# Reordering VectorE's sums in a seven-product projection, and moving the next image's GroupNorm statistics one attention group later

## The chip, the cores and the metric

One core of a Trainium2 chip. Its engines here are TensorE (matrix products, which it writes to the memory PSUM), VectorE (sums and products element by element), ScalarE (exponentials and copies) and GpSimd; transfers to and from the chip's main memory are called DMA. The metric is the device time of one execution in microseconds (us). All runs used here are within 1.5% of the fastest of their kernel and count as fast, at a granted TensorE clock of 0.995 to 0.999 of full speed. Numbers are medians of several executions unless they come from a trace, which is one execution; the span of a trace is about 2 us shorter than the time of the same execution.

## The reference, cut

Eight images of 512 x 32 x 32 in fp32. Each is normalised over groups of channels, goes through a 1x1 convolution, two blocks (3x3 convolution, attention with four heads over 1024 positions, 1x1 convolution), a final 1x1 convolution, and a residual sum.

```python
def bot_attention(x, qkv_w, rw, rh):
    qkv = conv2d(x, qkv_w, 0).reshape(b, 3, HEADS, HD, hw)
    q, k, v = (qkv[:, 0], qkv[:, 1], qkv[:, 2])
    r = (rw + rh).reshape(1, HEADS, HD, hw)                 # position sums
    logits = einsum('bhdi,bhdj->bhij', q, k + r) * HD ** -0.5
    out = einsum('bhij,bhdj->bhdi', softmax(logits), v)
# ...
x = x + conv_block(_gn(x), ...)                             # _gn: GroupNorm, the "statistics"
```

## The kernel before

The projection to q, k and v uses seven products of half-size blocks rather than eight (`project_strassen`), in 14 of the 16 blocks (images 1 to 7). Products go to PSUM; VectorE combines them. The part that matters is its end, where `ps_c`, `ps_d`, `ps_e` are PSUM tiles of a ring of three that the logits also use:

```python
product(ps_c, ps_w[:, 0], s2, t2)
tt(u[:, 0:2], ps_c, u[:, 0:2], ALU.add)
tt(u[:, 2], ps_w[:, 0], u[:, 2], ALU.add)
tt(k1, k1, u[:, 1], ALU.add)                      # reads no PSUM
add_r(0, 1)                                       # two position sums, read no PSUM
product(ps_d, ps_w[:, 1], s3, t3)
tt(k2, ps_d[:, 1], u[:, 1], ALU.add)
tt(q2, ps_d[:, 0], u[:, 0], ALU.add)
tt(v2, v_of(ps_w[:, 1]), v_of(u[:, 2]), ALU.add)
product(ps_e, ps_v[:, 0], block_qkv(n, 1, 1), t4)
tt(k3, k2, m5[:, 1], ALU.add)
tt(q3, q2, m5[:, 0], ALU.add)
tt(v3, v2, v_of(m5[:, 2]), ALU.add)               # reads no PSUM
tt(k2, k2, ps_e[:, 1], ALU.subtract)
freed = tt(q2, q2, ps_e[:, 0], ALU.subtract)      # last reader of ps_e
with tc.issue_after(freed.ins):
    tt(v1, v1, v_of(u[:, 2]), ALU.add)
    tt(v2, v2, v_of(ps_v[:, 0]), ALU.subtract)
    tt(q1, q1, u[:, 0], ALU.add)
def later():                                      # the other keys' position sums,
    for half in range(NH): add_r(1, half)         # done inside attention group 0
```

Attention runs in four groups (0 to 3) of eight blocks each: logits (TensorE), exponential (ScalarE), running sum of the exponentials for the softmax (`acc`, VectorE), product with v (TensorE, into `av_ps`, which has one buffer). At the end of a group the row sums go to `s_ps`; their reciprocal travels to memory and back to be spread over the partitions (`r_dram`, `rs`) and scales the output a group later. `behind[g]` is work put behind the first blocks of group g: in the first block of every image but the last, `ahead`:

```python
def ahead():
    g = next(groups)
    next(norm, None)      # a piece of the next image's GroupNorm: statistics, statistics, means, normalisation
    # ... loads
    if b == 0:            # image 0 also makes transformed weights for the second block
        if g == 0:
            make(1, 1, [2])
        elif g <= NM:
            make(1, 1, [0], [g - 1])   # the second of these ends with a store of 1 MB
# ...
scale(g, rs)              # ao *= rs, and then the next group's first output block may be read out
```

## Time and profile before

| | before |
|---|---|
| time, median of 6 runs beside the changed kernel | 2373.88 us (2373.83 to 2375.31) |
| span of the trace | 2371.5 us |
| TensorE busy | 2320.6 us (98%) |
| TensorE's waits that the change aims at | 14 x 0.65 in the projections, 6 x 1.01 at group 1 |
| image 0, first block: from its first projection matmul (71.89) to its first matmul after attention (171.5) | 99.6 us |

The prediction below shows the lines for the two waits. The 0.60 us that it counts for an operation is the usual distance between the starts of VectorE's TENSOR_TENSOR operations of 128x512 fp32 in its lines; each of them lasts 0.68 to 0.69 us there. One more place also belongs here, image 0. TensorE there, before, at the start of group 2; the columns are start, duration, engine, line, operation, and in brackets the idle time and what ended it:

```profile
128.92 3.51 PE L687 MATMUL av_ps<-pt,vT 64*64 64x512 f32 x16 [2.12 <-DVE ao L695]
```

and VectorE up to the start of group 3, where the scaling (L761) stands in its queue just before the read-out that TensorE waits for:

```profile
137.45 0.20 DVE L749 RECIPROCAL rc<-sums_all 128x8 f32<-128x8 f32 x1
...
143.90 0.69 DVE L761 TENSOR_TENSOR ao<-ao,rs 128x512 f32<-128x512 f32 x1
```

The block of 16 after the wait of 2.12 us takes 3.51 us rather than the usual 1.95; the granted clock was 0.58, 0.50, 0.50 and 0.71 in the four microseconds from 129.00. The time from the reciprocal to its use is 6.45 us, and TensorE, 1.6 us late from that slow stretch, doesn't wait at group 3 at all. Both facts return later.

### The profile page before, as it was taken

How to read it: one execution, taken by the hardware profiler on the slowest of the kernel's cores; microseconds unless marked ns; L12 is line 12 of the kernel's file. 1: busy time of each engine (PE TensorE's matmuls, PEld its weight loads, DVE VectorE, ACT ScalarE, POOL GpSimd, SP SyncE). 2: the span in 40 equal slices, each digit the busy share in tenths (PEclk: the TensorE clock that was granted, in tenths of full speed). 3: DMA queues.
4: the chain of work that ended last, by engine and by line, in shares of the span. 5: the costliest groups of instructions: out<-in, count | busy, mean ns of one | idle time of the engine just before them, and what ended most of it. 6: DMA issues, size and time to landing. Idle time of an engine off the chain costs nothing.

```text
span 2371.5 us, 36277 instructions
## 1 busy us (share of the span) xinstructions
PE 2320.6 (98%) x14794; PEld 1169.8 (49%) x14794; DVE 1753.1 (74%) x2811; ACT 946.3 (40%) x1246; POOL 88.2 (4%) x305
## 2 busy tenths in 40 slices
PE   7999999999999999999999999999999999999998
PEld 4536346363553636436364453635536354463633
DVE  8867778687786867868688676886767867677774
ACT  1442624435244352534425344253433525325252
POOL 1000000000100001000010000100001000000001
PEclk9999999999999999999999999999999999999999
DMA  7412234030430305303151131611207021160202
GB/s 251 152 53 89 95 104 194 15 129 15 148 151 15 130 15 186 117 10 129 33 212 74 31 108 33 257 33 54 86 28 262 28 85 55 34 228 16 85 11 69
DMA packets 93069, 226.39 MB, mean 95 GB/s; under 512 B 27872, under 2 KB 49312, under 8 KB 80224
## 3 DMA queue, kind: packets, MB, share of 16 engines
q1 hardware_dynamic: 81376, 174.71, 21.4%
q0 software_dynamic: 11520, 49.29, 5.2%
q8 instruction: 118, 1.93, 0.3%
q14 instruction: 55, 0.45, 0.1%
HBM read 190.41 MB, written 33.55 MB: 94 GB/s over the span
## 4 chain that ended last, share of the span: by engine, by line
PE 82%; DVE 14%; DMA 2%; issue 1%; ACT 0%; SPq 0%; DVEq 0%; POOL 0%; ACTq 0%
PE av_ps L687 16%; PE l_ps L661 14%; PE c_ps L879 13%; PE ps L343 10%; PE c L934 8%; PE c_new L934 6%; PE p_ps L556 5%; PE m_ps L900 5%; DVE acc L673 3%; PE pv_ps L560 2%; DVE st L443 1%; PE s_ps L705 1%; DVE acc L671 1%; DVE u_z L607 1%; DVE kr L577 1%
## 5 line engine op out<-in xcount | busy, mean ns | idle before, releaser
L665 ACT ACTIVATE pt<-l_ps 128x1024 f32<-128x1024 f32 x512 | 496.4, 1022 | 431.4 <-PE l_ps L661 420.1
L673 DVE TENSOR_TENSOR acc<-acc,pt 128x1024 f32<-128x1024 f32 x384 | 469.8, 1223 | 102.1 <-ACT pt L665 78.4
L687 PE MATMUL av_ps<-pt,vT 64*64 64x512 f32 x4096 | 486.6, 593 | 10.7 <-DVE ao L695 10.7
L661 PE MATMUL l_ps<-q,kr 64*64 64x512 f32 x4096 | 487.4, 591 | 9.1 <-DVE q L624 9.1
L879 PEld LDWEIGHTS c_ps<-v_in,u 128*128 128x128 f32 x2720 | 306.3, 192 | 7.9 <-issue 6.7
L879 PE MATMUL c_ps<-v_in,u 128*128 128x128 f32 x2720 | 306.9, 275 | 1.1 <-DVE v_in L400 1.1
L687 PEld LDWEIGHTS av_ps<-pt,vT 64*64 64x64 f32 x4096 | 152.1, 133 | 288.2 <-issue 221.2
L661 PEld LDWEIGHTS l_ps<-q,kr 64*64 64x64 f32 x4096 | 152.3, 133 | 283.4 <-issue 253.1
L343 PE MATMUL ps<-x,w 128*128 128x512 f32 x512 | 226.4, 598 | 2.2 <-DVE x L477 2.2
L343 PEld LDWEIGHTS ps<-x,w 128*128 128x128 f32 x512 | 96.7, 191 | 129.9 <-issue 126.6
L671 DVE TENSOR_TENSOR acc<-pt 128x1024 f32<-128x1024 f32 x64 | 78.3, 1223 | 64.7 <-ACT pt L665 64.7
L407 ACT COPY m<-c_ps 128x256 f32<-128x256 f32 x96 | 35.5, 370 | 224.7 <-PE c_ps L879 219.7
L934 PE MATMUL c_new<-t_in,ws 128*128 128x512 f32 x288 | 124.6, 592 | 0.0
L900 PE MATMUL m_ps<-ao,m_sb 128*128 128x512 f32 x256 | 112.5, 592 | 0.0
L328 ACT ACTIVATE m_kept<-m_kept,bh,sh 128x512 f32<-128x512 f32 x42 | 31.9, 806 | 146.0 <-DVE m_kept L1018 86.3
L761 DVE TENSOR_TENSOR ao<-ao,rs 128x512 f32<-128x512 f32 x64 | 44.1, 689 | 60.8 <-DMA rs<-r_dram 60.2
L934 PEld LDWEIGHTS c_new<-t_in,ws 128*128 128x128 f32 x288 | 54.7, 190 | 68.9 <-issue 66.0
L328 ACT ACTIVATE t<-m_ps,bh,sh 128x512 f32<-128x512 f32 x64 | 48.0, 776 | 83.9 <-PE m_ps L900 82.5
L556 PE MATMUL p_ps<-t_z,sq 128*128 128x512 f32 x168 | 81.3, 593 | 0.0
L372 POOL MEMSET w_rows<- 128x16 f32 x96 | 12.2, 128 | 1821.1 <-PE s_ps L705 1127.9
L900 PEld LDWEIGHTS m_ps<-ao,m_sb 128*128 128x128 f32 x256 | 48.6, 190 | 61.2 <-issue 61.2
L328 ACT ACTIVATE z<-z,bh,sh 128x512 f32<-128x512 f32 x64 | 48.6, 806 | 50.9 <-DVE z L436 50.9
(223 smaller groups left out, 2701.0 us busy)
## 6 DMA issues: line engine op xcount, KB each, us to landing
u<-u SPq DMA_DIRECT2D x85, 1024.0 KB
x<-in_x_dram SPq DMA_DIRECT2D x32, 512.0 KB
x_res<-in_x_dram POOLq DMA_DIRECT2D x28, 512.0 KB, 7.9
out_dram<-m_kept POOLq DMA_DIRECT2D x28, 512.0 KB, 7.4
w<-in_cv_w_dram SPq DMA_DIRECT2D x13, 1024.0 KB
u<-u_new POOLq DMA_DIRECT2D x12, 1024.0 KB, 6.0
rs<-r_dram SPq DMA_DIRECT2D x96, 128.0 KB
ws<-s SPq DMA_DIRECT2D x24, 512.0 KB
```

The source lines that it names most:

```text
L328: return nc.scalar.activation(dst, src, AF.Silu, scale=sh[:, k : k + 1], bias=bh[:, k : k + 1])
L343: nc.tensor.matmul(ps[:, half, :], w_of(k), rhs_of(k, half), start=(k == begin), stop=(k == end))
L556: nc.tensor.matmul(ps[:, o, :], w[:, o, :], rhs, start=not onto, stop=True, skip_group_check=onto)
L560: nc.tensor.matmul(v[:, ts(j, P)], rhs[:, ts(j, P)], w[:, 2, :], start=j == 0 and not onto, stop=True, skip_group_check=True,)
L661: nc.tensor.matmul(ps[kh * HD : (kh + 1) * HD, hd, :], kr[r, c, o : o + HD], q[r, c, ts(half, HALF)], start=True, stop=True,)
L665: exp = nc.scalar.activation(pt[:, i], ps, AF.Exp, scale=SCALE)
L671: return nc.vector.tensor_tensor(accs[g], pt[:, 0], pt[:, 1], ALU.add)
L673: ins = nc.vector.tensor_tensor(accs[g], accs[g], pt[:, i], ALU.add)
L687: nc.tensor.matmul(avs[g][hd * HD : (hd + 1) * HD, kh, :], vT[r, j, o : o + HD], pt[r, i, hd, :], start=(j == 0), stop=(j == NJ - 1),)
L879: nc.tensor.matmul(ps[:, row, col, :], us[i][:, k, row, SLOT[col], :], vs[i][:, k, row, col, :], start=(k == 0), stop=(k == NM - 1),)
L900: nc.tensor.matmul(pss[oc][:, half, :], m2_sb[:, n, k, ts(oc, P)], ao[:, k, ts(half, HALF)], start=(k == 0), stop=(k == NM - 1),)
L934: nc.tensor.matmul(ps[:, o, :], w[:, k, ts(o, P)], rhs[part][:, c, :], start=(k == 0 and not onto), stop=(k == KB - 1), skip_group_check=onto,
```

## The change

Intent: let the last reader of `ps_e` come as early as possible, so that the logits find their PSUM tile free; and take the statistics out of group 0, where VectorE has the postponed position sums to do, to group 1 and 2, with the means in the middle of group 2. No operation is added or removed.

```diff
             tt(u[:, 2], ps_w[:, 0], u[:, 2], ALU.add)
-            tt(k1, k1, u[:, 1], ALU.add)
-            add_r(0, 1)
             ps_d = big()
# ...
             tt(q3, q2, m5[:, 0], ALU.add)
-            tt(v3, v2, v_of(m5[:, 2]), ALU.add)
             tt(k2, k2, ps_e[:, 1], ALU.subtract)
             freed = tt(q2, q2, ps_e[:, 0], ALU.subtract)
             with tc.issue_after(freed.ins):
+                tt(v3, v2, v_of(m5[:, 2]), ALU.add)
+                last = tt(v2, v2, v_of(ps_v[:, 0]), ALU.subtract)
+            with tc.issue_after(last.ins):
+                tt(k1, k1, u[:, 1], ALU.add)
+                add_r(0, 1)
                 tt(v1, v1, v_of(u[:, 2]), ALU.add)
-                tt(v2, v2, v_of(ps_v[:, 0]), ALU.subtract)
                 tt(q1, q1, u[:, 0], ALU.add)
# ... attention: work may also be put behind a later pair of blocks
-                    if j0 == 0:
-                        with tc.issue_after(added.ins):
-                            behind.get(g, lambda: None)()
+                    with tc.issue_after(added.ins):
+                        behind.get(g if j0 == 0 else (g, j0 // PAIR), lambda: None)()
# ... ahead()
-            next(norm, None)
+            if g > 0:
+                next(norm, None)
# ...
+        behind[NG - 2, 2] = lambda: next(norm, None)
```

## The prediction

> **What bounds the kernel now.** I read the page first, then the waits of TensorE, then the timeline of TensorE and VectorE around the places where TensorE waits.
>
> ```profile
> span 2371.5 us, 36277 instructions
> ...
> PE 2320.6 (98%) x14794; PEld 1169.8 (49%) x14794; DVE 1753.1 (74%) x2811; ACT 946.3 (40%) x1246; POOL 88.2 (4%) x305
> ```
>
> TensorE is busy for 2320.6 of 2371.5 us, at a granted clock of 0.997. The change takes no matmul away, so all it can win is idle time of TensorE: 50.9 us, 2.1% of the span. A gain of over 2% is nearly excluded by this line alone. The waits of TensorE name the idle time:
>
> ```profile
> PE gm_ps L449 <- DVE mv L444: 11.8, 1, 11.8
> PE av_ps L687 <- DVE ao L695: 10.7, 11, 2.1
> PE l_ps L661 <- DVE q L624: 9.1, 14, 0.7
> ```
>
> (Columns: microseconds in total, times, longest.) The first is the start of the program and stays. The other two are what the change aims at. The third comes once in each of the 14 projections that use seven products (images 1 to 7, two each). Of the second, the timeline shows six of exactly 1.01 us, always where group 1 of attention follows group 0 in an image that prepares a next one (images 1 to 6, first block); three in image 0 (0.49, 2.12 and 0.63); and two after slow transfers (0.63, 0.77).
>
> Image 2, TensorE at the end of the projection:
>
> ```profile
> 679.93 1.05 PE L560 MATMUL pv_ps<-qkv_sb,t_z 128*128 128x128 f32 x8
> 680.92 1.95 PE L661 MATMUL l_ps<-q,kr 64*64 64x512 f32 x16
> 683.51 1.95 PE L661 MATMUL l_ps<-q,kr 64*64 64x512 f32 x16 [0.65 <-DVE q L624]
> 685.28 1.90 PE L687 MATMUL av_ps<-pt,vT 64*64 64x512 f32 x16
> 687.00 1.90 PE L661 MATMUL l_ps<-q,kr 64*64 64x512 f32 x16
> ```
>
> and VectorE there:
>
> ```profile
> 676.65 0.68 DVE L609 TENSOR_TENSOR kr<-kr,u_z 128x512 f32<-128x512 f32 x1
> 677.37 0.69 DVE L577 TENSOR_TENSOR kr<-kr,rw_sb 128x512 f32<-128x512 f32 x1
> 677.98 0.68 DVE L615 TENSOR_TENSOR kr<-p_ps,u_z 128x512 f32<-128x512 f32 x1
> 678.58 0.68 DVE L578 TENSOR_TENSOR kr<-kr,rh_sb 128x512 f32<-128x512 f32 x1
> ...
> 681.58 0.68 DVE L622 TENSOR_TENSOR vT<-vT,m_z 128x512 f32<-128x512 f32 x1
> 682.18 0.68 DVE L623 TENSOR_TENSOR kr<-kr,p_ps 128x512 f32<-128x512 f32 x1
> 682.78 0.68 DVE L624 TENSOR_TENSOR q<-q,p_ps 128x512 f32<-128x512 f32 x1
> ```
>
> The reader is to see a buffer wait, not a data wait. The second block of logits writes a PSUM tile (three rotate) whose last reader is the subtraction of L624, which ends at 683.46; the block starts at 683.51. Ahead of that reader stand four operations that read no PSUM tile that anyone waits for: L609, L577, L578 and L622. Undisturbed blocks of 16 follow each other by 1.72 us (685.28, 687.00), here the distance is 2.59 and the next one 1.77, so the stall costs 2.59 + 1.77 - 2 x 1.72 = 0.92 us, more than the 0.65 of the wait row, which subtracts a modelled end.
>
> Boundary of groups 0 and 1 in the same image, VectorE then TensorE:
>
> ```profile
> 691.38 1.88 DVE L443 BATCH_NORM_STATS2 st<-x 128x6 f32<-128x512 f32 x3
> ...
> 700.09 0.68 DVE L695 TENSOR_TENSOR ao<-av_ps,ao 128x512 f32<-128x512 f32 x1
> ```
>
> ```profile
> 699.18 0.64 PE L705 MATMUL s_ps<-acc,ones 128*32 128x256 f32 x8
> 700.83 1.95 PE L687 MATMUL av_ps<-pt,vT 64*64 64x512 f32 x16 [1.01 <-DVE ao L695]
> ```
>
> The attention output has one PSUM buffer, so group 1 waits until L695 has read group 0's. VectorE comes late because group 0 holds both the postponed sums of the keys (L577 and L578, four operations, 2.4 us) and the first statistics (2.7 us). Where nothing delays, the output block follows the sums by 0.57 us (730.36 to 730.93), here by 1.65: 1.08 us lost, six times.
>
> [...]In a run of such operations the starts lie 0.60 us apart, so I count 0.60. [...]the trace has 4.9 to 5.4 us from reciprocal to use as a rule, and 6.4 to 6.5 three times.
>
> **The change, part one: projections.** Nothing is added or removed; VectorE has the same 0.60 us operations. I walk the new order from the third product's sums, which end at 677.25 or so. The next sum (second half's k) now comes at once but has to wait for its product: TensorE's four matmuls from 675.60 last until 677.48, so it starts at 677.52. Then at 0.60 each: q 678.12, v 678.72 (its product ends at 678.37), k3 679.32, q3 679.92, k minus product five 680.52 (that ends at 680.09), q minus it 681.12, end about 681.80. The buffer is free 1.66 us earlier than 683.46, and TensorE wants it at 680.92 + 1.72 = 682.64. The stall goes: 0.92 x 14 = 12.9 us.
>
> What may come in its place: the keys of the second half are now finished last. v3 681.72, v2 682.32, k1 682.92, v1 683.52, first position sum 684.12, q1 684.72, second position sum 685.32 to 686.00. The third block of logits needs it and would start at 687.00 - 0.92 = 686.08. By the built order that matmul indeed has a new wait on exactly this operation. The margin is under 0.1 us; I allow 0 to 0.1 a stage, 0.7 us in all. The exponentials are safe: the buffer that v3 frees is needed near 684.0.
>
> **Part two: statistics.** Group 0 of images 1 to 6 loses 2.7 us of VectorE work. The accumulations then start at 685.92 instead of 685.18; pair 0 1.23, pair 1 2.47, postponed sums 2.41, pairs 2 and 3 about 5.0, group 1's first 1.14: L695 runs from 698.17 to 698.85. TensorE will want it at 699.75 - 0.92 = 698.83. So the 1.08 us go, 6 x 1.08 = 6.5, less up to 0.1 for this thin margin. The margin is the same in the eight projection stages without statistics, where no wait was: up to 0.1 each, 0.7 expected over all 14.
>
> Group 1 had statistics before and has them still. Group 2 gets 2.7 us that it did not have and loses the means (0.7) from its start. In the trace VectorE idles 1.33 us before the third pair there, so its reciprocal comes 0.65 us later (2.7 - 0.7 - 1.33). In images 1 to 6 the slack from reciprocal to use is 6.45 us against the usual 5.1, so it is absorbed, except after a slow transfer: 0.3 expected. The means move one and a half groups later but the normalisation in group 3 stays put; their inputs are ready near 721 where TensorE asks at 725. Nothing.
>
> Image 0 has weights to make besides. Its group 0 wait of 0.49 goes and its 2.12 shrinks by about 0.6, while group 2's reciprocal comes 1.65 later and may cost 0.3 to 1.2 there: +0.3 net.
>
> Sum: 12.9 - 0.7 + 6.5 - 0.7 - 0.3 + 0.3 = 18.0. I take off 1 more, because three of the margins are below the 0.1 us to which I know the starts: 17 us, and 2374.0 - 17 = 2357.
>
> **The rivals.**
> First, the wait moves instead of going: from L624 to the second position sum of the first keys. For it: the new wait in the built order, the tiny margin. Against it: even if VectorE is 0.3 us later than I count, it costs 0.3 of 0.92. That would give 14 x 0.3 = 4 us back: 2361.
> Second, VectorE is the bound of all group 0 and the boundary wait stays or appears in all 14 stages, since the accumulations start 0.74 us later against a TensorE that is 0.92 ahead. At 0.3 us each, about 4 us; with the first, 2365.
> Third, the added statistics in group 2 make the reciprocal late and TensorE waits at group 3. For it: image 0's 2.12 us arose just so, in a group with statistics and weights. If images 1 to 6 lost 1 us each: 2363.
> Fourth, nothing changes because TensorE's idle is absorbed later by a transfer. Against it: no TensorE wait on a DMA is in the list; the gain carries to the end.
>
> **Range and chances.** All rivals together give back about 14 of 18 us, which is 2370; that is unlikely at once. The best case without any of my deductions is 2354. The range is 2352 to 2366. Over 2% faster would need 47 us, nearly all idle time with the start: 0.01. Over 2% slower needs a disorder that nothing here hints at: 0.01. Within 2%: 0.98.
>
> **What would show it.** Right: TensorE's wait on the q subtraction is gone from its list, 14 times; the six waits of 1.01 at group 1 are gone; TensorE's busy time stays within 1 us of 2320.6 and its idle time falls by about 17. Wrong: a row of 14 waits of the logits on the position sum (rival one), of the output block on L695's successor 14 times (two), or six near group 3 (three). A changed busy time of TensorE, or a wait on a transfer, would mean that I looked in the wrong place.

## The result, and the profile after

| | before | after |
|---|---|---|
| time, median of 6 runs each | 2373.88 us | 2368.32 us (2366.99 to 2370.37) |
| ratio | | 0.9977, 95% interval 0.9964 to 0.9989 |
| span of the trace | 2371.5 us | 2365.4 us |

Ratios here are the mean time of one kernel's fast runs over that of the other's of the same rounds, so not quite the ratio of the medians quoted. The kernel became 5.6 us faster, within 2% as foreseen; 17 us had been predicted, and 2368.3 lies outside the range of 2352 to 2366.

The page of the changed kernel, first its span and the busy time of the engines:

```profile
span 2365.4 us, 36291 instructions
...
PE 2321.6 (98%) x14794; PEld 1181.0 (50%) x14794; DVE 1751.7 (74%) x2811; ACT 944.5 (40%) x1246; POOL 87.9 (4%) x305
```

TensorE's busy time moved by 1.0 us only, so idle time is where to look. Its waits (total, times, longest):

```profile
PE gm_ps L449 <- DVE mv L444: 11.6, 1, 11.6
PE av_ps L688 <- DVE ao L696: 10.7, 20, 3.9
```

The row of 14 waits of the logits on the subtraction is gone, as intended. But the output block's row, which should have lost its six waits of 1.01 us, has the same total as before: 20 waits rather than 11, the longest 3.9 rather than 2.1. The timeline of TensorE around one projection (image 1, second block) shows the short ones:

```profile
528.94 3.66 PE L662 MATMUL l_ps<-q,kr 64*64 64x512 f32 x32
532.43 1.90 PE L688 MATMUL av_ps<-pt,vT 64*64 64x512 f32 x16
534.38 1.95 PE L662 MATMUL l_ps<-q,kr 64*64 64x512 f32 x16
...
546.56 0.64 PE L706 MATMUL s_ps<-acc,ones 128*32 128x256 f32 x8
547.36 1.95 PE L688 MATMUL av_ps<-pt,vT 64*64 64x512 f32 x16 [0.15 <-DVE ao L696]
```

and VectorE in the same stretch shows why:

```profile
529.75 0.69 DVE L623 TENSOR_TENSOR vT<-vT,m_z 128x512 f32<-128x512 f32 x1
530.54 0.69 DVE L624 TENSOR_TENSOR vT<-vT,pv_ps 128x512 f32<-128x512 f32 x1
531.14 0.69 DVE L626 TENSOR_TENSOR kr<-kr,u_z 128x512 f32<-128x512 f32 x1
...
533.55 0.69 DVE L578 TENSOR_TENSOR kr<-kr,rh_sb 128x512 f32<-128x512 f32 x1
...
546.62 0.69 DVE L696 TENSOR_TENSOR ao<-av_ps,ao 128x512 f32<-128x512 f32 x1
```

Two things are to be seen. First, the starts of L623 and L624 are 0.79 us apart where the others are 0.60: L624 (`v2 -= ps_v`) overwrites what L623 (`v3 = v2 + m5`) reads, and in the built program it waits on a semaphore for L623 (the trace has an instruction of 0.02 us for this wait at L624, 14 times). Everything behind it is 0.19 late, so the last position sum L578, which the third block of logits needs, starts at 533.55, and that block starts at 534.38: 1.95 after its predecessor, where 1.72 is undisturbed, so 0.23 lost. Second, VectorE has no idle time from there to L696, and the output block follows the row sums by 0.80 us (546.56 to 547.36) where 0.57 is undisturbed: another 0.23. This second loss happens in all 14 projection blocks.

Image 0 holds the longest wait. TensorE at the start of group 3, after:

```profile
147.89 3.39 PE L688 MATMUL av_ps<-pt,vT 64*64 64x512 f32 x16 [3.89 <-DVE ao L696]
```

The chain of waits there (start, duration, what):

```profile
138.70 0.12 DVE rc L750
...
138.84 4.25 DMA r_dram<-rc
...
143.62 2.83 DMA rs<-r_dram
```

and GpSimd's queue:

```profile
137.86 0.53 POOL L1095 DMA_DIRECT2D u<-u_new  x1 [33.40 <-DVE u_new L304]
```

This last is the store of 1 MB of transformed weights. The reciprocal's tiny transfer is issued just after it and takes 4.25 us. From reciprocal (138.61) to use (146.54) it is 7.93 us, against 6.45 before. The reciprocal is 1.16 us later than before, because group 2 now has statistics besides the weights (and 0.57 of it because all of image 0 starts that much later in this trace); and TensorE comes to the boundary 1.58 us earlier (its row sums start at 143.36, before 144.94). So VectorE's answer is 146.54 - 143.90 = 2.64 later to a TensorE that is 1.58 earlier: a margin that was a little positive became a wait of 3.89 us.

Setting whole stages against each other, by the starts of TensorE's matmuls in the two traces, gives the account of the 6.1 us between the spans:

| part | predicted gain | measured gain |
|---|---|---|
| block without statistics (8 of them), each | 0.8 to 0.9 | 0.36 (133.70 to 133.34) |
| block with statistics (images 1 to 6), each | about 1.9 | 1.49 (156.38 to 154.89); image 2 only 0.65 |
| images 1 to 7 together | 17.7 | 11.1 (first to last matmul after attention: 2169.3 to 2158.2; image 0's second block lies in this stretch, unchanged at 138.25) |
| image 0 | +0.3 | 3.2 lost (99.61 to 102.86) |
| start before image 0, and end after image 7 | 0 | 0.6 and 1.2 lost |

The last row is scatter: over the twelve traces of this study (ten experiments and the two kernels) the first projection matmul of image 0 starts between 70.3 and 72.5 us, and the stretch behind the last matmul after attention takes between 30.7 and 34.2; nothing in the change lies in either.

### The profile page after: what moved, and what is told of

Its sections match the earlier page's. It is cut to its first block, busy times and chain, and to the rows that moved or that the text cites. A ratio compares the mean times of both kernels' runs of the same rounds, so it can differ in the third digit from the quotient of the medians.

```text
span 2365.4 us, 36291 instructions
## 1 busy us (share of the span) xinstructions
PE 2321.6 (98%) x14794; PEld 1181.0 (50%) x14794; DVE 1751.7 (74%) x2811; ACT 944.5 (40%) x1246; POOL 87.9 (4%) x305
## 4 chain that ended last, share of the span: by engine, by line
PE 89%; DVE 6%; DMA 2%; ACT 2%; issue 1%; SPq 0%; POOL 0%; DVEq 0%; ACTq 0%
PE av_ps L688 16%; PE l_ps L662 15%; PE c_ps L879 14%; PE ps L343 12%; PE c L934 8%; PE p_ps L556 7%; PE c_new L934 6%; PE m_ps L900 5%; PE pv_ps L560 3%; DVE acc L674 2%; ACT pt L666 1%; PE p_ps L560 1%; DVE acc L672 1%; PE s_ps L724 1%; DMA rs<-r_dram 1%; PE s_ps L706 1%
## 5 line engine op out<-in xcount | busy, mean ns | idle before, releaser
L688 PEld LDWEIGHTS av_ps<-pt,vT 64*64 64x64 f32 x4096 | 157.1, 133 | 284.0 <-issue 216.7
L662 PEld LDWEIGHTS l_ps<-q,kr 64*64 64x64 f32 x4096 | 158.2, 133 | 269.6 <-issue 255.4
L407 ACT COPY m<-c_ps 128x256 f32<-128x256 f32 x96 | 35.4, 369 | 224.9 <-PE c_ps L879 219.8
```

The source lines that it names most:

```text
L662: nc.tensor.matmul(ps[kh * HD : (kh + 1) * HD, hd, :], kr[r, c, o : o + HD], q[r, c, ts(half, HALF)], start=True, stop=True,)
L688: nc.tensor.matmul(avs[g][hd * HD : (hd + 1) * HD, kh, :], vT[r, j, o : o + HD], pt[r, i, hd, :], start=(j == 0), stop=(j == NJ - 1),)
```

## The experiments

Edits are given against the changed kernel. "A" is the account in the section above: the parts depend on each other through VectorE's queue in group 0, and the rest was lost to the neighbours' wait, to the full queue at group 1, and to image 0. "B" is in each case the rival that the piece under test isn't the cause; the expectations spell it out. The kernel before ran beside every one of them (medians 2373.86 to 2374.39).

### The two parts alone

Projection order alone: statistics in groups 0 and 1 as before.

```diff
-                    with tc.issue_after(added.ins):
-                        behind.get(g if j0 == 0 else (g, j0 // PAIR), lambda: None)()
+                    if j0 == 0:
+                        with tc.issue_after(added.ins):
+                            behind.get(g, lambda: None)()
# ...
-            if g > 0:
-                next(norm, None)
+            next(norm, None)
# ...
-        behind[NG - 2, 2] = lambda: next(norm, None)
```

> The kernel before with the new order of the projections alone; statistics where they were. Theory A (VectorE's queue, not the buffer, is the bound from the third product of the projection to the end of group 0 of attention, so the two halves of the change depend on each other): in the changed kernel the accumulations start 0.94 us later against TensorE's clock than before; with the statistics still in group 0 the wait of 1.01 us at group 1 grows by about that in images 1 to 6, so 6 x 0.94 = 5.6 us are lost there, and the 8 projections without statistics gain 0.37 each (3.0): 2373.9 + 2.6 = 2376.5 us. Theory B (the halves simply add, each projection gains its own part): 14 x 0.37 to 0.62 us gained, 2365 to 2369 us.

Measured: 2380.06 us (10 runs), ratio 1.0025 (1.0016 to 1.0035). The projection order alone makes the kernel slower by 6.2 us. TensorE in image 2 at group 1:

```profile
700.73 0.64 PE L706 MATMUL s_ps<-acc,ones 128*32 128x256 f32 x8 [1.52 <-DVE acc L674]
702.38 1.95 PE L688 MATMUL av_ps<-pt,vT 64*64 64x512 f32 x16 [1.00 <-DVE ao L696]
```

Where there was one wait of 1.01 there are now two, because VectorE does the three displaced sums later and still has the statistics. The direction was A's; the size was larger than A's number. In images 4 and 6 the block with statistics takes 157.32 us, 0.94 more than before, just as A had it. In images 1, 3 and 5 it takes 158.9 to 159.0: in image 1 the output block after the two waits takes 3.41 us rather than 1.95, and the granted clock was 0.69, 0.50, 0.50 and 0.61 in the four microseconds from 410.00, 3.4 us at half in all. That images 3 and 5, with the same block time, lost their 1.6 to 1.7 us in the same way is an estimate; three times that is more than the 3.6 us by which A fell short.

Statistics alone: the projection as before.

```diff
             tt(u[:, 2], ps_w[:, 0], u[:, 2], ALU.add)
+            tt(k1, k1, u[:, 1], ALU.add)
+            add_r(0, 1)
# ...
             tt(q3, q2, m5[:, 0], ALU.add)
+            tt(v3, v2, v_of(m5[:, 2]), ALU.add)
             tt(k2, k2, ps_e[:, 1], ALU.subtract)
             freed = tt(q2, q2, ps_e[:, 0], ALU.subtract)
             with tc.issue_after(freed.ins):
-                tt(v3, v2, v_of(m5[:, 2]), ALU.add)
-                last = tt(v2, v2, v_of(ps_v[:, 0]), ALU.subtract)
-            with tc.issue_after(last.ins):
-                tt(k1, k1, u[:, 1], ALU.add)
-                add_r(0, 1)
                 tt(v1, v1, v_of(u[:, 2]), ALU.add)
+                tt(v2, v2, v_of(ps_v[:, 0]), ALU.subtract)
```

> The kernel before with the statistics moved alone; projections in the old order. Theory A: the six waits of 1.01 us at group 1 go (6 x 1.08 = 6.5 us), the 14 waits of 0.65 us on the q subtraction stay, no wait of 0.15 at group 1 appears, image 0 loses about 3.3 to 3.9 us at group 3: about 2373.9 - 6.5 + 3.6 = 2371 us. Theory B, with the projections worth 5 to 9 us of the 5.6 measured: the statistics are worth nothing or less, 2374 to 2377 us.

Measured: 2373.53 us (13 runs), ratio 0.9997 (0.9989 to 1.0006): no difference, and as a time between the two expectations. The waits of TensorE say more:

```profile
PE av_ps L687 <- DVE ao L695: 9.3, 6, 4.2
PE l_ps L661 <- DVE q L624: 9.0, 14, 0.6
```

The six waits of 1.01 are gone and the 14 of the logits are back. Images 1 to 7 gained 5.7 us (2163.6 from 2169.3), and image 0 lost 4.6 (104.2), among others to its longest wait of 4.2 and to 6.8 us of half clock that began 1.3 us before its end (granted clock 0.64 in the microsecond from 145.00, 0.50 in the next six, 0.95 in the last).

So alone the parts are worth +6.2 and -0.3 us, together -5.6: 11.5 us better than their sum. The new projection order moves three sums (1.8 us), which VectorE did while it waited for a product, to behind the products and so towards group 0; only with the statistics out of that group is there room.

### Image 0

Image 0's statistics in groups 0 and 1 as before, all else changed:

```diff
-            if g > 0:
+            if g > 0 or b == 0:
                 next(norm, None)
# ...
-        behind[NG - 2, 2] = lambda: next(norm, None)
+        if b > 0:
+            behind[NG - 2, 2] = lambda: next(norm, None)
```

> The changed kernel, but image 0 keeps the statistics in groups 0 and 1 and the means at the start of group 2. Theory A: the stall of 3.89 us at group 3 of image 0 is what the added statistics did there (reciprocal late, its transfer behind the 1 MB store of transformed weights); it goes, the waits of about 0.5 and 2.1 us at groups 1 and 2 come back: 2368.3 - 3.3 = 2365 us. Theory B: image 0's stall is a chance of the transfers: 2368 us, with a similar stall in image 0.

Measured: 2363.29 us (5 runs), ratio 0.9954 (0.994 to 0.9967), 5.0 us faster than the changed kernel; image 0 is 99.8 us long again. A holds: nearly half of the missing 11 us was lost in one image of eight. The changed kernel's own trace shows 3.1 us of it there (102.86 to 99.76). The five other traces with image 0's statistics moved and the store issued as before (statistics alone, gap, keys first, half later, store later) take 104.2 to 104.6 us in image 0. In the changed kernel's trace there is one stretch of half clock there, of 3.41 us; with the statistics alone it is 6.8 us, and with the gap twice 3.4 us (129.3 to 132.7 and 149.8 to 153.2, by the granted clock of each microsecond). Of the other three the timelines show the slow blocks: behind the two waits 2.48 and 3.13, 2.41 and 2.87 us rather than 1.9 (keys first; half later within 0.04 of these), and 3.69 and 2.41 behind the second (store later).

Is it the store? First the store of the weights was put behind the statistics of group 3 in program order:

```diff
-                if k == NM - 1:
+                if k == NM - 1 and (n, oc, i) != (1, 1, 0):
                     nc.gpsimd.dma_start(u_dram[n][oc][i], us[oc, i])
# ... ahead(), b == 0, g == 3
+                else:
+                    nc.gpsimd.dma_start(u_dram[1][1][0], us[1, 0])
```

> The changed kernel; in image 0 alone the 1 MB store of transformed weights that is issued 1.0 us before the reciprocal's transfer in group 2 goes out in group 3 instead. Theory A (that transfer is slow because it shares the engines with the store: 7.9 us from reciprocal to use against 4.9 to 5.4 elsewhere): the stall at group 3 of image 0 falls from 3.9 us to 1.0 to 1.5, and with it the half clock of the following microseconds (1.6 us) may not come: 2368.3 - 2.5 to 4 = 2364.3 to 2365.8 us. Theory B (the transfer is late only because the reciprocal is): the stall stays over 3 us, 2368 us.

Measured: 2368.29 us (9 runs), ratio 0.9974. This run failed as a test. The trace shows the store issued at 137.26: nothing ahead of it in its queue held it, so the later line changed nothing. Program order is no time. The second attempt gives the store something to wait for, a multiplication of one element by 1.0 on VectorE in group 3:

```diff
+                else:
+                    one = us[1, 0][:, 1, 1, 3, P - 1 : P]
+                    nc.vector.tensor_scalar(one, one, 1.0, None, ALU.mult)
+                    nc.gpsimd.dma_start(u_dram[1][1][0], us[1, 0])
```

> The changed kernel again with the 1 MB store of image 0 sent out in group 3, now held there by a real dependency: one VectorE operation in group 3 multiplies one element of the weights by 1 (0.2 us), and the store needs it. (Without one, in the run before, the store was issued as early as ever.) Theory A (the reciprocal's transfer is slow because the store fills the transfer engines): from reciprocal to use 5 to 6.4 us instead of 7.9; the stall at group 3 of image 0 falls from 3.9 us to 1.0 to 2.4; with it the 1.7 us of half clock may go: 2368.3 - 1.5 to 4.5 = 2364 to 2367 us. Theory B (slow for itself): 7.9 us and 2368 us.

Measured: 2362.26 us (5 runs), ratio 0.995 (0.9936 to 0.9963), 6.1 us faster than the changed kernel. The chain of waits, then TensorE at groups 2 and 3:

```profile
137.18 3.06 DMA r_dram<-rc
...
140.78 2.98 DMA rs<-r_dram
```

```profile
127.01 3.00 PE L688 MATMUL av_ps<-pt,vT 64*64 64x512 f32 x16 [1.79 <-DVE ao L696]
...
145.20 1.95 PE L688 MATMUL av_ps<-pt,vT 64*64 64x512 f32 x16 [1.49 <-DVE ao L696]
```

With the store out of the way (issued at 147.97) the transfer takes 3.06 rather than 4.25 us. From reciprocal (136.96) to use (143.85) it is 6.89 us rather than 7.93: B is out, but A's 5 to 6.4 is not reached either. The run before agrees: there, with the store issued 0.98 us ahead, it is 4.84 us from the issue of the transfer to that of the next, which waits for it (138.24 to 143.08). The store isn't all, for in group 1 of the changed kernel the same kind of transfer takes 1.41; what else slows it these runs don't show.

The wait is 1.49 rather than 3.89 us, but not all of this is the store's doing. Counted from image 0's first projection matmul (70.88 here, 72.46 in the changed kernel), VectorE's answer comes 1.11 us earlier and TensorE comes 1.30 later: in this execution its half clock fell behind the wait at group 2 (3.00 us for the first block above; granted clock 0.88, 0.50, 0.50, 0.50 and 0.91 in the microseconds from 127.00), and in the changed kernel behind the one at group 3 (147.45 to 150.86). Image 0 is 100.3 us long, 2.5 shorter than in the changed kernel. So the collision with the store is shown, and about 1.1 us as its price on the path; the rest of the 2.5 goes with the place of the half clock, of which more below. How the remainder of the 6.1 us between the medians divides is not shown. The profiled execution was the slowest of five (2364.49), the changed kernel's 1.1 us below its median, and the spans differ by 2.7.

### The neighbours' wait

The first keys' sum is put between `v3` and `v2 -= ps_v`, and `v1` ahead of the position sums (where it already ran in the trace of the changed kernel):

```diff
             with tc.issue_after(freed.ins):
-                tt(v3, v2, v_of(m5[:, 2]), ALU.add)
+                v_3 = tt(v3, v2, v_of(m5[:, 2]), ALU.add)
+            with tc.issue_after(v_3.ins):
+                k_1 = tt(k1, k1, u[:, 1], ALU.add)
+            with tc.issue_after(k_1.ins):
                 last = tt(v2, v2, v_of(ps_v[:, 0]), ALU.subtract)
             with tc.issue_after(last.ins):
-                tt(k1, k1, u[:, 1], ALU.add)
-                add_r(0, 1)
                 tt(v1, v1, v_of(u[:, 2]), ALU.add)
+                add_r(0, 1)
                 tt(q1, q1, u[:, 0], ALU.add)
```

> The changed kernel with one pair of operations exchanged in each projection: k1's sum now stands between v3 = v2 + m5 and v2 = v2 - product, which writes what v3 reads. The trace of the changed kernel shows 0.79 us from start to start there against 0.60 elsewhere. Theory A (all of VectorE's queue to the end of group 0 is the bound): the 0.19 us go and TensorE gains all of it at the two waits, 14 x 0.19 = 2.7 us: 2365.6 us; the third logits block's lateness of 0.2 us and the 0.15 at group 1 both fall. Theory B (the 0.19 us are read latency that is paid elsewhere): 2368 us.

Measured: 2365.73 us (5 runs), ratio 0.9961 (0.9947 to 0.9975). VectorE:

```profile
532.08 0.68 DVE L623 TENSOR_TENSOR vT<-vT,m_z 128x512 f32<-128x512 f32 x1
532.68 0.68 DVE L625 TENSOR_TENSOR kr<-kr,u_z 128x512 f32<-128x512 f32 x1
533.29 0.68 DVE L627 TENSOR_TENSOR vT<-vT,pv_ps 128x512 f32<-128x512 f32 x1
```

All three are 0.60 or 0.61 apart: with another operation between them the dependent pair costs nothing extra. All of the gain is at the third block of logits, which is now 0.04 late; the wait at group 1, which A wanted to see fall, stays at 0.15. The block without statistics takes 133.14 rather than 133.34 us, the one with 154.69 rather than 154.89: 0.20 a block, the size of the 0.19 that was taken away. The median is 2.6 us lower, as 14 x 0.19 = 2.7 would have it, though its interval overlaps the changed kernel's, so the block times are the better evidence. (In the trace images 1 to 7 together are only 0.9 us shorter, 2157.3 from 2158.2; 1.7 us lost to half clock in image 0's second block, told below, falls into that stretch.)

### The full queue at group 1

Next, the keys' sums were moved as far forward as they go, which removes the wait of the third block of logits altogether:

```diff
             with tc.issue_after(last.ins):
-                tt(k1, k1, u[:, 1], ALU.add)
-                add_r(0, 1)
-                tt(v1, v1, v_of(u[:, 2]), ALU.add)
+                img_k = img(k1)
+                k_2 = tt(img_k, img_k, rw_sb[...], ALU.add)
+            with tc.issue_after(k_2.ins):
+                v_1 = tt(v1, v1, v_of(u[:, 2]), ALU.add)
+            with tc.issue_after(v_1.ins):
+                k_3 = tt(img_k, img_k, rh_sb[...], ALU.add)
+            with tc.issue_after(k_3.ins):
                 tt(q1, q1, u[:, 0], ALU.add)
# (k1's sum between v3 and v2, as in the experiment before)
```

> The kernel of the gap experiment (2365.7 us), and the sums of the second half's keys moved further ahead, before v1 and q1; the amount of VectorE work is the same. Theory A (VectorE's queue is full to the end of group 0, only its length counts): what the third block of logits gains, 0.06 us a stage, comes back as a longer wait at group 1: 2365.7 us, unchanged, the 14 waits at group 1 at 0.15 to 0.2 us. Theory B (the new wait of the logits on the keys is a cost of its own): 14 x 0.06 to 0.1, about 1 us faster: 2364.7 us. A difference of this size may stay below the noise of about 1.5 us; the trace decides by the waits at group 1.

Measured: 2365.9 us (5 runs), ratio 0.9961 (0.9947 to 0.9975), the same as without it. TensorE at group 1:

```profile
549.68 1.95 PE L695 MATMUL av_ps<-pt,vT 64*64 64x512 f32 x16 [0.25 <-DVE ao L703]
```

The third block of logits now comes without delay, but the wait at group 1 is 0.25 rather than 0.15, in all 14 blocks, and the block time stays at 133.14. TensorE's earlier arrival was turned into a longer wait for VectorE, which is the bound from the projection to group 1. So work must leave that stretch. Half of the postponed position sums go to the last pair of group 1:

```diff
-            def later():
-                for half in range(NH):
-                    add_r(1, half)
+            def later(half):
+                add_r(1, half)
# ...
                         if i == 1 and later is not None:
-                            later()
+                            later(0)
+                        if i == 2 * NQ - 1 and later is not None:
+                            later(1)
# (and the gap of the experiment before last)
```

> The kernel of the gap experiment (2365.7 us), and the second half of the postponed position sums (two operations, 1.2 us) goes from group 0 to the last pair of group 1, where VectorE idles about 1.2 to 1.5 us. Theory A: with 1.2 us less in the queue of group 0 the waits at group 1 go in all 14 stages, 0.22 us each from start to start: 3.1 us, 2362.6 us. Theory B (the waits at group 1 come from ScalarE's copy or from the sums' matmul, not from VectorE's queue): 2365.7 us, the waits of 0.15 remain.

Measured: 2364.01 us (5 runs), ratio 0.9954 (0.9941 to 0.9968), between the expectations. TensorE at the same place:

```profile
548.70 0.64 PE L707 MATMUL s_ps<-acc,ones 128*32 128x256 f32 x8
549.27 1.09 PE L689 MATMUL av_ps<-pt,vT 64*64 64x512 f32 x8
```

No bracket: the output block follows the row sums by 0.57, and so in all 14. The block without statistics takes 132.92, again 0.22 less, which is the loss of 0.23 read off the changed kernel. Of the blocks with statistics three gained about 0.22 and image 5's 0.16; image 6's lost 0.04 and image 2's 0.54, since they wait at group 2 instead (in image 2 for 1.56 us). The trace confirms A; the time alone would not have decided.

### Together

All of it: gap, keys first, half later, image 0 as before.

> Everything together: changed kernel, keys first without the adjacent pair, half of the postponed sums in group 1, image 0 with the statistics where they were before. Theory A: 2368.3 - 2.7 - 3.1 - 3.3 to 5.0 (measured for image 0: 5.0) = 2357.5 to 2359.2 us. Theory B (these gains are the same idle time counted twice): not under 2362 us, which is about what the best single step gave.

Measured: 2355.26 us (5 runs, 2354.69 to 2356.94), ratio 0.9922 (0.9909 to 0.9936). Blocks take 132.82 and 154.37 us, and the spans fall by 12.3 from the changed kernel. This is faster than both kernels, by 13 and 19 us, and 2 us better than A expected.

In a last run image 0's weights, which stayed in groups 1 and 2 so far, were also made a group later, in 2 and 3:

```diff
-                elif g <= NM:
-                    make(1, 1, [0], [g - 1])
+                elif g > 1:
+                    make(1, 1, [0], [g - 2])
```

> The kernel with everything together (2355.3 us); in image 0 the two portions of transformed weights move from groups 1 and 2 to groups 2 and 3, so group 1 has the statistics alone. Theory A (a group holds about one of these jobs of 2.7 to 3 us before its reciprocal is late): the wait of 1.98 us at group 2 goes, the one at group 3 stays about 2, and group 3, which normalises the next image (3 us) and now makes weights too, may end 1 to 2 us late: 2353 to 2356 us. Theory B (image 0's waits are set by transfers alone): 2355.3 us with the same waits.

Measured: 2355.11 us (5 runs), ratio 0.9918 (0.9904 to 0.9931): no difference from the run before that these counts could show. In the trace the wait of 1.98 at group 2 is gone, as A said and B did not. Image 0's first block is 97.1 rather than 99.9 us long, with waits of 0.49 and 1.22 and no block of 16 longer than 1.95, but that execution began it 1.6 us later, and the stretch behind the last matmul after attention took 3.2 us more.

## Why the prediction was wrong in size and right in direction

By the two traces 10.9 of the 17 us are missing: 6.6 in images 1 to 7 (17.7 predicted, 11.1 measured), 3.5 in image 0 (0.3 to be gained, 3.2 lost) and 1.8 of scatter at the two ends, less the 1 us that had been deducted.

**The stall of the logits, 14 x 0.92 = 12.9, less 0.7.** The buffer came free as worked out, and the row of 14 waits vanished. The step that failed is the walk through the new order at 0.60 us an operation: "v3 681.72, v2 682.32". These two neighbours are 0.79 apart. The lines quoted in the prediction had a warning, L609 and L577 at 676.65 and 677.37: two operations on the same keys, 0.72 apart. With a margin of "under 0.1 us", 0.19 was enough: the third block of logits came 0.23 late. The first rival named exactly this (0.3 a block, 4 us) and was undervalued. (The walk also begins with a misreading: the third product's sums end at 676.73, not at 677.25. It has no effect, because the next sum waits for its product until 677.52.) Removing the adjacency gave 0.20 a block back.

**"Up to 0.1" a block at group 1, 0.7 in all.** Mis-sized: 0.23 in all 14 blocks, 3.2 us. The second rival described it, and the sign named for it, 14 waits of the output block, came. From the sum that waits for the fourth product (525.55) to that boundary VectorE has no idle time, so each small excess adds up: the 0.19, a first accumulation of 1.33 rather than 1.23 (534.15 to 535.48; the trace before had 1.32 there already), four that take 5.12 rather than "about 5.0". In a queue without a gap such excesses can't be judged one by one, each as below 0.1; their sum decides. Moving one pair of sums out of the stretch removed the loss, and removing the earlier wait only made this one longer.

**Together:** of the predicted 0.92 a block, about 0.30 was lost at the third logits (0.62 measured between the first and fourth blocks of logits, 9.52 to 8.90) and 0.26 at group 1, which leaves the measured 0.36. Over 14 blocks that is 14 x 0.56 = 7.8 us, of which 1.4 were allowed for.

**The statistics, 6 x 1.08 = 6.5.** Right: blocks with statistics gained 1.49 - 0.36 = 1.13 more than those without. Run alone this part gained 5.7 us in images 1 to 7. In image 2, waits of 0.82 and 0.60 after late scalings ate 0.84; the prediction had 0.3 for such things. (Its "6.4 to 6.5 three times" is misread: the trace has 6.45 from reciprocal to use at 22 of 48 places, where VectorE is busy until then, and 5.0 to 5.6 as a rule where it waits for the transfer. No sum rests on it.)

**Image 0, "+0.3 net".** This step failed. It was right that the 0.49 would go; the 2.12 shrank to 1.86, not by 0.6. The later reciprocal was foreseen, "0.3 to 1.2", but against a TensorE in its old place; TensorE came 1.58 earlier, and the transfer fell behind the store of the weights and took 4.25. Waits of 1.86 + 3.89 = 5.75 replaced 0.49 + 2.12 = 2.61, and image 0 lost 3.2 us in this trace, 4.6 to 5.0 in five others. The third rival (late reciprocal at group 3) happened here, and in images 1 to 6 only in image 2, with 0.60 us. Putting image 0's statistics back gave 5.0 us.

**The clock.** The prediction left it out. In the attention of image 0 both kernels' traces have one stretch of half clock of 3.41 us (129.17 to 132.58 before, 147.45 to 150.86 after), and the blocks of 16 take 3.51 and 3.39 us, but the place differs. Behind group 2, as before, it delays TensorE to where it would have waited at group 3 anyway (image 0 as before: 3.64 us for the block behind group 2, no wait at group 3, 99.8 us; all together: 1.95 us for that block, a wait of 1.98 at group 3, 99.9 us); behind group 3 it comes on top. It moves these runs by up to 1.7 us at a time (5.40 for 3.70 us below). The first projection matmuls of image 0's second block come after the same wait of 1.18 us in every kernel (with one of 0.62 some 2 us earlier), untouched by the change. In the changed kernel and then in the one with the gap:

```profile
224.00 3.70 PE L343 MATMUL ps<-z,qkv_sb 128*128 128x512 f32 x8 [1.18 <-ACT z L328]
```

```profile
224.83 5.40 PE L343 MATMUL ps<-z,qkv_sb 128*128 128x512 f32 x8 [1.17 <-ACT z L328]
```

and one microsecond of the latter (after the busy time and count of each engine: the granted clock, the DMA share, GB/s):

```profile
226.00:227.00 1.00, 1.00 (x3) 0.48 (x2) 0.00 (x0) 0.99 (x2) 0.00 (x0) 0.50 0.00 0
```

The same eight matmuls take 3.70 us in seven of the twelve traces and 5.40 in five (the gap, keys first, half later, all together, store held). With the gap the table shows half clock over them, at a cost of 1.70 us; for the other four of the five it is read off the same 5.40. What tells the two apart was looked for in three traces: by the clock records of the kernels before and after, and by the table of microseconds for the gap. From 60 us on and up to 45 us before the end, the stretches of half clock are these:

| trace | half clock | distance of the ends |
|---|---|---|
| before | 64.31 to 67.73, 129.17 to 132.58 | 64.85 = 19 x 3.413 |
| after | 65.53 to 68.94, 147.45 to 150.86 | 81.92 = 24 x 3.413 |
| gap, those in the table | 129.3 to 132.74, 149.8 to 153.22, 224.9 to 228.32 | 20.48 = 6 x 3.413, 75.10 = 22 x 3.413 |

Each lasts 3.41 us (to 0.02 with the gap), and within a trace the ends lie whole multiples of that apart. With the traces before and after cut into pieces of 3.41 us at these ends, half clock followed the pieces in which TensorE was idle for 2.37 and 2.12 us (before), 1.88 and 3.41 us (after); no other piece of full clock was followed by it, and the most idle of those had 1.17 us (before) and 1.70 us (after). With the gap the waits of 0.62 and 1.17, together 1.79, fall into one piece (221.50 to 224.91), and half clock came; in the changed kernel an edge at 222.54 parts them, and none came. So in these traces it goes with where the pieces lie whether such waits cost 1.7 us more, and their place differs from trace to trace. That the same decides in the other traces is an estimate. It fits the projection order alone: in image 1 TensorE was idle for 2.4 of the 3.4 us before the half clock at 410.4.

**The rest.** "No TensorE wait on a DMA" held by the list's wording only: the wait is on VectorE, which waits on the transfer. The range was too narrow: it rested on margins known to 0.1 us, and treated rivals as separate that a single full queue ties together.

## What to carry to other kernels

When operations are moved out of one tight stretch, add up the work of the engine over the whole stretch up to the next point where another engine needs it; if it never idles there, a saving before it turns into a wait at its end until some work leaves the stretch (here the wait at group 1 grew from 0.15 to 0.25 us and the block time stayed at 133.14, until half of the postponed sums left). When walking a queue by hand, charge more for an operation that depends on the one right before it (here 0.72 and 0.79 us from start to start rather than 0.60), and put an independent one between them (here 0.60 and 0.61 again). Look at the image that differs from the rest by itself: a change that is right for seven of eight can lose in the first what it gains in the others.
